# A four-layer graph network on one core: the attention of batch 13 is put behind the scores of batch 14

## The chip, the core and the metric

The kernel runs on one core of a Trainium2 chip. A core has a matrix engine (PE, with its weight loads PEld), a vector engine (DVE), an activation engine (ACT), a general engine (POOL) and a synchronizing engine (SP), which here only issues transfers. Each engine takes its instructions in the order in which the program lists them; between engines, semaphores say what has to wait for what. Transfers are issued from SP and from POOL and are run by 16 DMA engines. The metric is the device time in microseconds (us) of one execution; given is the median of several.

## The reference, cut to what matters

128 graphs of 128 nodes with 128 features pass through four graph layers, each `x = x + layer(relu(layernorm(x)), adj, ...)`. The change concerns the first layer only:

```python
D = jnp.abs(x[:, :, None, :] - x[:, None, :, :])
h = jnp.einsum('bijc,oc->bijo', D, W1) + b1
m = jnp.mean(h, axis=(0, 1, 2)); v = jnp.mean((h - m) ** 2, axis=(0, 1, 2))
h = _leaky((h - m) / jnp.sqrt(v + EPS) * g1 + be1)
s = jnp.einsum('bijo,uo->biju', h, W2)[..., 0] + b2[0]
A = jax.nn.softmax(jnp.where(A_init > 0, s, NEG), axis=-1)
y = jnp.einsum('bij,bjc->bic', A, x) @ Wg.T + bg
mg = jnp.mean(y, axis=(0, 1)); vg = jnp.mean((y - mg) ** 2, axis=(0, 1))
y = _leaky((y - mg) / jnp.sqrt(vg + EPS) * gg + beg)
out = jnp.concatenate([x, y], axis=2) @ Wt.T + bt
```

For every pair of nodes of a graph a hidden vector is computed and normalized over all pairs of all graphs; its score goes through a softmax over the neighbours. The result `y` is normalized over all nodes of all graphs. So there are two points at which everything before must be done: the statistics of `h`, and those of `y`. The three layers that follow are graph attention layers without such a point.

## The kernel before, in words

The two statistics cut the kernel into three stages.

**Stage one** computes, for each graph, the hidden values of all pairs (tile `v`, 128 x 4064) and their statistics, and stores `v` in DRAM; the last eight graphs' stay on the chip.

**Stage two**, where the change is, works in batches of eight graphs (`GS`): 16 batches, of which batch 15 comes first (its `v` are on the chip), and then 0 to 14. So batch 13 is the last but one, and batch 14 the last. A batch has these parts:

- `graph_scores`, for each graph: load `v` (L677, SP queue, 2 MB), affine and leaky on two halves of it (L657 on ACT, then L428 on DVE), a relu `r` of its last quarter (L664, ACT), and ten products on PE (L702) that add the graph's scores into the batch's PSUM tile `sc`. A graph's products come after those of the graph before; the last one's end is the event `("scores", k)`.
- `score_table`: it waits for that event. DVE copies `sc` to `us` (L721, two instructions), POOL issues four transfers of it to DRAM (`s<-us`, L731), and then one that reads it back in another layout (`u<-s`, L742), which waits for the four to land. Then two chains of `attention` are started, one for each four graphs (`GB`; called A and B here).
- `edges`, for each four graphs: load the adjacency (`adj`, L753, POOL queue) and the hidden features (`ht`, L761, SP queue), make the mask `negm` (L757, DVE), count edge types (L774, ACT), and `zg`, the features times Wg (`pz` on PE, L765, copied by ACT, L768).
- `attention`: one addition on POOL (L784); six products into `pl` (L791 to L794, PE; the last takes `negm`); maximum and difference (`mx`, `e`, L799 and L801, DVE); exp (L803, ACT); sum, reciprocal and scaling (`sm`, `ri`, `e`, L806 to L809, DVE); transposes `pt` (L813, PE), copied to `eT` (L816, ACT); products with `zg` into `py` (L820, PE); bias into `yt` (L823, ACT); a store of `yt` (L825, POOL queue); its statistics (L830 and L831, DVE).

When all batches' statistics are there, `y_norm` makes `y_sc` and `y_bi` (L382 to L420). `edge_types` puts the number of edge types seen into `types` (L849 to L857). After the stage every engine reads `types` and branches on it (L1349); SP can do so as soon as `types` is written, as it has nothing else to do, and then issues the first loads of the third stage (L1030).

**Stage three** computes the rest of layer one and layers two to four, four graphs at a time. Each group's first step applies `y_sc` and `y_bi` to the loaded `y` (`yl`, L1139).

**What sets the order.** Each part is a generator that yields its next step with the engine, an estimate of its duration, and the buffers that it takes and frees. `in_order` walks through all parts that are under way (up to ten in stage two) with a clock of its own: of all steps that could go next it takes the one that could begin first by its estimates, and of equals the part that was started first (once all parts have been started: the one started last). The order in which it takes them is the order of each engine's instructions, and stays fixed. A step can yield `"after"` with the name of an event: it is then not taken before this event is there, by the planner's clock. This is no wait on the chip by itself; it only moves the step in the lists. The transfers of SP and of POOL stand in the lists of these engines in the same way.

By this order, PE's list in the tail of stage two reads: scores of batch 14, graphs 0 to 4; `pl` of batch 13, A; graph 5; `pl` of batch 13, B; graph 6; a `pz`; graph 7; then the rest of batch 13's attention, and batch 14's.

Of the kernel before, what the change touches and what calls it, by code (L numbers as in the profile page):

```python
# [24 lines left out]
GS = 8  # L25
GB = 4
# [129 lines left out]
def bcast(ap, pos, n):  # L156

    dims = [list(d) for d in ap.ap]
    return bass.AP(tensor=ap.tensor, offset=ap.offset, ap=dims[:pos] + [[0, n]] + dims[pos:])
# [3 lines left out]
def kernel(ctx: ExitStack, tc: tile.TileContext, x, adj, w, out):  # L163
    nc = tc.nc
    NB = x.shape[0]
# [267 lines left out]
    with tc.tile_pool(name="h_pool", bufs=1) as h_pool, tc.tile_pool(name="pairs", bufs=B_V) as b_v:  # L433
# [193 lines left out]
        with tc.tile_pool(name="b2", bufs=2) as b2p, tc.tile_pool(name="b_s", bufs=2, space=PSUM) as b_s, tc.tile_pool(  # L627
            name="b_ps", bufs=6, space=PSUM
        ) as b_ps:
            scores, masks = {}, {}  # L630
# [80 lines left out]
            def score_table(k):  # L711

                yield "after", ("scores", k)
                yield DVE, 1.6, "us", "sc"
                sc = scores.pop(k)
                sd = scores_d[k % 2]
                us = b2p.tile([P, 512], F32, tag="us", name="us")
                for s in range(2):
                    n = 8 * width[2 * s]
                    half = slice(64 * s, 64 * s + 64)  # L720
                    nc.vector.tensor_scalar(  # L721
                        us[half, 0:n], sc[half, 0:n], b2_rows[half, :], None, ALU.add
                    )
                yield POOL, 2.6, "u u", ""
                u = b2p.tile([P, GS, W], F32, tag="u", name="u")
                for q in range(NQ):
                    skewed = bass.AP(
                        tensor=sd.tensor, offset=sd.offset + QR * q * ROW + 1,
                        ap=[[W + 1, QR], [4 * ROW, 8], [1, width[q]]],
                    )  # L730
                    nc.gpsimd.dma_start(  # L731
                        skewed,
                        us[QR * q : QR * q + QR, 0 : 8 * width[q]].rearrange(
                            "p (r j) -> p r j", r=8
                        ),
                    )
                yield "wait", 3.0
                yield POOL, 1.2, "", "us"
                by_row = bass.AP(
                    tensor=sd.tensor, offset=sd.offset, ap=[[ROW - 1, P], [W + 1, GS], [1, W]]  # L740
                )
                nc.gpsimd.dma_start(u, by_row)  # L742
                yield "wait", 8.0
                for g in range(GS // GB):
                    yield "fork", attention(k * GS // GB + g, u[:, g * GB : g * GB + GB, :])
                yield "join",

            def edges(g):
# [29 lines left out]
                if not to_see:  # L778
                    yield "done", "types"

            def attention(g, u):
                flat = "p g j -> p (g j)"
                yield POOL, 0.6, "", ""
                nc.gpsimd.tensor_tensor(  # L784
                    u[:, :, 0 : W - P], u[:, :, 0 : W - P], u[:, :, P:W], ALU.add
                )
                yield "after", ("edges", g)
                yield PE, 3.0, "pb", "u negm"
                negm, zg = masks.pop(g)
                pl = b_ps.tile([P, GB, P], F32, tag="pb", name="pl")  # L790
                nc.tensor.matmul(pl, ident, u[:, :, 0:P], start=True, stop=False)  # L791
                for i in range(GB):
                    nc.tensor.matmul(pl[:, i, :], u[:, i, 0:P], ident, start=False, stop=False)
                nc.tensor.matmul(  # L794
                    pl.rearrange(flat), ident, negm.rearrange(flat), start=False, stop=True
                )
                yield DVE, 1.4, "e", "pb"
                mx = b2p.tile([P, GB], F32, tag="mx", name="mx")
                nc.vector.tensor_reduce(mx, pl, AX.X, ALU.max)  # L799
                e = b2p.tile([P, GB, P], F32, tag="e", name="e")  # L800
                nc.vector.tensor_tensor(e, pl, bcast(mx, 2, P), ALU.subtract)  # L801
                yield ACT, 0.65, "", ""
                nc.scalar.activation(e, e, AF.Exp)  # L803
                yield DVE, 1.7, "", ""
                sm = b2p.tile([P, GB], F32, tag="sm", name="sm")
                nc.vector.tensor_reduce(sm, e, AX.X, ALU.add)  # L806
                ri = b2p.tile([P, GB], F32, tag="ri", name="ri")
                nc.vector.reciprocal(ri, sm)
                nc.vector.tensor_tensor(e, e, bcast(ri, 2, P), ALU.mult)  # L809
                yield PE, 0.7, "pb", "e"  # L810
                pt = b_ps.tile([P, GB, P], F32, tag="pb", name="pt")
                for i in range(GB):
                    nc.tensor.transpose(pt[:, i, :], e[:, i, :], ident)  # L813
                yield ACT, 0.65, "eT", "pb"
                eT = b2p.tile([P, GB, P], F32, tag="eT", name="eT")
                nc.scalar.copy(eT, pt)  # L816
                yield PE, 1.0, "pb", "eT zg"
                py = b_ps.tile([P, GB, P], F32, tag="pb", name="py")
                for i in range(GB):
                    nc.tensor.matmul(py[:, i, :], zg[:, i, :], eT[:, i, :], start=True, stop=True)  # L820
                yield ACT, 0.7, "yt", "pb"
                yt = b2p.tile([P, GB, P], F32, tag="yt", name="yt")
                nc.scalar.activation(yt, py, AF.Identity, bias=bg)  # L823
                yield POOL, 0.7, "", ""
                nc.gpsimd.dma_start(y_d[g], yt)  # L825
                yield "done", ("stored", g)
                yield DVE, 1.5, "", "yt"
                y6 = b2p.tile([P, GB, 6], F32, tag="y6", name="y6")
                for i in range(GB):
                    nc.vector.bn_stats(y6[:, i, :], yt[:, i, :])  # L830
                nc.vector.bn_aggr(y_mv[:, g, :], y6.rearrange("p a b -> p (a b)"))  # L831
                to_norm.remove(g)
                if not to_norm:
                    yield "done", "y"
# [37 lines left out]
            ]  # L872
            makers = []

            for k in [NB // GS - 1, *range(NB // GS - 1)]:
                of_edges = [partial(edges, k * GS // GB + g) for g in range(GS // GB)]
                order = sorted(range(GS * k, GS * k + GS), key=lambda b: b not in here)
                of_graphs = [partial(graph_scores, order, i) for i in range(GS)]

                n = 0 if makers else 2  # L880
                makers += of_graphs[:n] + of_edges + of_graphs[n:] + [partial(score_table, k)]
# [484 lines left out]
def program(arrays):  # L1366

    import concourse.bacc as bacc

    nc = bacc.Bacc("TRN2", target_bir_lowering=False, num_devices=1)  # L1370
    ins, aps = {}, {}
    for name in ["x", "adj"] + _WEIGHTS:
        a = arrays[name]
        ins[f"in_{name}"] = a
        aps[name] = nc.dram_tensor(
            f"in_{name}", a.shape, mybir.dt.from_np(a.dtype), kind="ExternalInput"
        ).ap()
    out = nc.dram_tensor("out_0", arrays["x"].shape, F32, kind="ExternalOutput").ap()
    with tile.TileContext(nc) as tc:
        kernel(tc, aps["x"], aps["adj"], aps, out)  # L1380
    return nc, ins
# [10 lines left out]
```

## Time and profile before

| | us |
|---|---|
| median of the runs | 3127.03 |
| lowest and highest of the three runs | 3125.08, 3133.86 |
| the profiled execution, its own time | 3131.72 |
| its span, first to last instruction | 3129.9 |
| stage two: first score product | 1257.8 |
| last score product of batch 14 ends | 2014.6 |
| `y_bi` done, stage three begins | 2052.0 |

The profile has start times from the start of the span. Each line of a timeline gives start, duration, engine, source line, operation, output and input, how many instructions are merged in the line, and in brackets how long the engine had been idle before it and what released it. Line numbers (L791) are those of the kernel before. The chain that ended last is followed back from the last instruction, at each step to what released it; in it, a name such as `DMA u<-s` stands for the time in which a transfer was waited for, and "issue" for time in which an engine waited for nothing that the profile shows. A clock of 1.00 is the full TensorE clock.

Busy over the span: PE 91%, DVE 85%, ACT 84%, POOL 48%. These shares are means over three stages with different limits, so they don't say what an edit at the end of the second is worth.

### The profile page before, as it was taken

The numbers are of one execution on the slowest core, as the hardware profiler recorded it, in microseconds if no ns is written. First come the engines' busy times: TensorE is split into PE (matmuls) and PEld (weight loads), VectorE is DVE, ScalarE is ACT, GpSimd is POOL, SyncE is SP. The second block draws the span as 40 slices with busy tenths as digits, with TensorE's granted clock in tenths as the row PEclk, the third lists the DMA queues.
The fourth block names the chain that finished last, engine by engine and source line by source line (L and its number), as shares of the span: only waits on it lengthen the run. The fifth ranks groups of instructions, "written<-read, shape, count | busy, mean of one in ns | idle before, by whom it ended". The sixth has DMA issues, their size and how long they took to land. (4 is left out here: it accounts for less than half of the span.)

```text
span 3129.9 us, 47376 instructions
## 1 busy us (share of the span) xinstructions
PE 2852.8 (91%) x17526; PEld 1588.3 (51%) x17577; DVE 2656.4 (85%) x4730; ACT 2626.3 (84%) x3050; POOL 1494.6 (48%) x953
## 2 busy tenths in 40 slices
PE   6999999999999999787988888879999999999997
PEld 2444434333443333233333333367877777787776
DVE  6999999999999999776877877667787787787886
ACT  4999999999999998887877878657777877787786
POOL 5999999999999997111111111121222222222202
PEclk8999999999999999898999999989999999999999
DMA  3555555555555651899999999620111111111000
GB/s 120 241 239 240 242 239 244 227 227 244 236 227 228 252 224 41 351 393 381 402 405 406 397 409 400 227 75 11 45 48 35 48 38 45 41 38 42 18 1 22
DMA packets 150722, 606.53 MB, mean 194 GB/s; under 512 B 15633, under 2 KB 99026, under 8 KB 119762
## 3 DMA queue, kind: packets, MB, share of 16 engines
q1 hardware_dynamic: 140242, 569.86, 46.0%
q0 software_dynamic: 10240, 33.53, 3.0%
q8 instruction: 143, 2.34, 0.3%
q14 instruction: 97, 0.79, 0.1%
HBM read 322.74 MB, written 280.61 MB: 193 GB/s over the span
## 5 line engine op out<-in xcount | busy, mean ns | idle before, releaser
L552 POOL TENSOR_TENSOR d<-he 128x2016 f32<-128x2016 f32 (+1 forms) x288 | 1021.6, 3573 | 68.1 <-PE ph L569 62.2
L569 PE MATMUL ph<-d,w1T 128*64 128x512 f32 (+1 forms) x4096 | 927.5, 595 | 36.5 <-DVE d L549 17.6
L555 ACT ACTIVATE d<-d 128x2016 f32<-128x2016 f32 (+1 forms) x352 | 675.0, 1921 | 13.1 <-POOL d L552 13.0
L584 DVE BATCH_NORM_STATS2 six<-v 128x6 f32<-128x512 f32 (+1 forms) x1024 | 624.6, 670 | 5.6 <-ACT v L579 5.4
L569 PEld LDWEIGHTS ph<-d,w1T 128*64 128x64 f32 x4096 | 308.0, 136 | 546.2 <-issue 397.3
L579 ACT COPY v<-ph 128x1008 f32<-128x1008 f32 (+1 forms) x512 | 509.6, 1028 | 30.7 <-PE ph L569 27.9
L549 DVE TENSOR_TENSOR d<-he,pt 128x2048 f32<-128x2048 f32 (+1 forms) x224 | 505.5, 2257 | 2.6 <-PE ph L569 2.3
L939 POOL TENSOR_TENSOR rs<-ve,nhalf 128x4 f32<-128x4 f32 x96 | 119.1, 1241 | 738.6 <-DVE ve L936 480.4
L428 DVE SCALAR_TENSOR_TENSOR v<-v 128x1528 f32<-128x1528 f32 x256 | 434.0, 1742 | 34.2 <-ACT v L657 33.5
L657 ACT ACTIVATE v<-v,h_bi,h_sc 128x1528 f32<-128x1528 f32 x256 | 413.2, 1664 | 6.7 <-DVE h_bi L420 6.7
L702 PE MATMUL sc<-v,w_slide 128*32 128x512 f32 (+1 forms) x1536 | 322.6, 601 | 17.2 <-DVE v L428 16.9
L1095 PE MATMUL pa<-vals,p 128*128 128x99 f32 (+2 forms) x2048 | 253.2, 279 | 11.3 <-DVE p L966 7.7
L1095 PEld LDWEIGHTS pa<-vals,p 128*128 128x128 f32 x2048 | 248.5, 197 | 29.1 <-DVE p L966 11.3
L702 PE MATMUL sc<-v,w_line 128*32 128x504 f32 x512 | 261.0, 592 | 0.0
L702 PE MATMUL sc<-r,w_relu 128*32 128x504 f32 x512 | 259.1, 588 | 0.0
L966 DVE SCALAR_TENSOR_TENSOR p<-p,q 128x1024 f32<-128x1024 f32 (+1 forms) x192 | 206.7, 1083 | 48.5 <-ACT q L1082 24.4
L569 PE MATMUL ph<-both,us 128*64 128x512 bf16 x1920 | 236.4, 379 | 0.0
L569 PEld LDWEIGHTS <-us 128*64 128x64 bf16 x1920 | 124.4, 110 | 147.5 <-issue 91.6
L1081 ACT ACTIVATE p<-z 128x1024 f32<-128x1024 f32 x128 | 133.2, 1041 | 35.2 <-PE z L962 34.8
L664 ACT ACTIVATE r<-v,h_bi,h_sc 128x1008 f32<-128x1008 f32 x128 | 157.6, 1231 | 0.0
L702 PEld LDWEIGHTS sc<-v,w_slide 128*32 128x32 f32 x1536 | 65.1, 109 | 160.1 <-DVE v L428 83.3
L803 ACT ACTIVATE e<-e 128x512 f32<-128x512 f32 x32 | 20.2, 631 | 141.0 <-DVE e L801 141.0
(255 smaller groups left out, 4505.4 us busy)
## 6 DMA issues: line engine op xcount, KB each, us to landing
v<-v SPq DMA_DIRECT2D x240, 2032.0 KB, 8.9
xg<-in_x SPq DMA_DIRECT2D x64, 256.0 KB, 3.0
ht<-h SPq DMA_DIRECT2D x64, 256.0 KB, 6.3
u<-s POOLq DMA_DIRECT2D x16, 768.0 KB, 11.7
h<-he SPq DMA_DIRECT2D x32, 256.0 KB, 2.6
adj<-in_adj SPq DMA_DIRECT2D x32, 256.0 KB, 2.9
adj<-in_adj POOLq DMA_DIRECT2D x32, 256.0 KB, 7.5
y<-yt POOLq DMA_DIRECT2D x32, 256.0 KB, 6.2
```

The lines of the kernel that those rows point to most:

```text
L428: engine.scalar_tensor_tensor(out, v, slope, v, ALU.mult, ALU.max)
L549: nc.vector.tensor_tensor(dv, later, own, ALU.max if larger else ALU.subtract)
L552: nc.gpsimd.tensor_tensor(dv, later, own, ALU.subtract)
L555: nc.scalar.activation(d[:, 0 : 4 * n], d[:, 0 : 4 * n], AF.Abs)
L569: nc.tensor.matmul(ph[64 * a : 64 * a + 64, t, 0:n], wt, x_, start=part == 0, stop=not larger or part == 3,)
L579: nc.scalar.copy(v.rearrange("p (t e) -> p t e", t=2), ph[:, :, 0:n])
L584: nc.vector.bn_stats(made["six"][:, 2 * q + t, :], v[:, t * n : t * n + n])
L657: nc.scalar.activation(part, part, AF.Identity, bias=h_bi, scale=h_sc)
L664: nc.scalar.activation(made["r"][:, 0:n], part, AF.Relu, bias=h_bi, scale=h_sc)
L702: nc.tensor.matmul(sc[rows, 0:n], wz[:, 31 - k : 63 - k], z, start=begins and q < NQ, stop=ends and q != NQ - 1, tile_position=(0, rows.st ...
L966: nc.vector.scalar_tensor_tensor(p, p, FLOOR, q, ALU.max, ALU.max)
L1095: nc.tensor.matmul(pa_all[:, h * (DH + 1) : h * (DH + 1) + n], p[:, h, :], vals_all[:, e : e + n], start=True, stop=True,)
```

## The change

`attention` now gets the number of its batch. For the last batch but one in the order of the list (`batches[-2:-1]`, batch 13) its first step yields `"after"` with the event `("scores", 14)`. The planner then takes no step of batch 13's two attention chains before it has taken the last score product of batch 14.

```diff
-                    yield "fork", attention(k * GS // GB + g, u[:, g * GB : g * GB + GB, :])
+                    yield "fork", attention(k, k * GS // GB + g, u[:, g * GB : g * GB + GB, :])
...
-            def attention(g, u):
+            def attention(k, g, u):
                 flat = "p g j -> p (g j)"
+                if k in batches[-2:-1]:
+
+                    yield "after", ("scores", batches[-1])
                 yield POOL, 0.6, "", ""
...
-            for k in [NB // GS - 1, *range(NB // GS - 1)]:
+            batches = [NB // GS - 1, *range(NB // GS - 1)]
+            for k in batches:
```

What this does to the engines' lists, all in the tail of stage two:

- PE: the score products of batch 14's graphs 5, 6 and 7 now come without a gap behind those of graph 4. Behind them come `pl` A, `pl` B, a `pz`, `pt` A, the small transpose of `edge_types`, the other `pz`, `py` A, `pt` B, `py` B, and then batch 14's `pl`, as before.
- DVE: the 14 `v` instructions of graphs 1 to 7 now come without a gap, then the two `us`, and only then `negm`, `mx`, `e` and the rest of batch 13's attention. `types` now comes behind `us` and behind `e` of B.
- ACT: one exchange: `eT` of A now stands ahead of `exp` of B.
- POOL: batch 14's `u<-s` now stands ahead of the store of batch 13's `yt` A, and batch 14's two additions ahead of the store of `yt` B.
- SP: the early load of `y` for stage three's first group and one load of `ht` change places.

The lists of stage one and of stage three are the same as before.

## The prediction

> **What bounds the kernel now.** I read first the busy times by stage (busy us and instruction counts of PE, PEld, DVE, ACT, POOL; then granted clock, DMA share, GB/s).
>
> ```profile
> 1257.80:2052.00 794.20, 664.00 (x3585) 271.87 (x3585) 590.80 (x654) 629.47 (x573) 117.76 (x175) 0.92 0.94 372
> 2052.00:3129.90 1077.90, 1004.64 (x7437) 823.39 (x7488) 851.30 (x2304) 830.21 (x1472) 238.98 (x320) 0.97 0.12 36
> ```
>
> Stage two is bound by its loads of v (DMA 0.94), but the last of them is issued at 1978, so its tail is not. I therefore went to the chain that ended last (start, us, what), around the end of stage two:
>
> ```profile
> 1997.32 1.05 PE pl L791 x2
> ...
> 2003.65 1.05 PE pl L791 x2
> ...
> 2009.97 1.09 PE pz L765 x8
> 2011.06 3.52 PE sc L702 x17
> ...
> 2020.85 0.43 issue
> 2021.28 8.63 DMA u<-s
> ...
> 2030.76 2.08 PE pl L791 x2
> ```
>
> Batch 13's `pl` and a `pz` stand between the last three graphs' `sc` products of batch 14. When those end (2014.58), batch 14's table still has to go to DRAM and back, and PE starts its attention only at 2030.76. Stage three waits for all of it: every `yl` needs `y_bi`, at 2051.99. The timelines of ACT, DVE and POOL say what else could hold the last products:
>
> ```profile
> 2001.16 3.23 ACT L657 ACTIVATE v<-v,h_bi,h_sc 128x1528 f32<-128x1528 f32 x2
> ...
> 1998.65 3.58 DVE L428 SCALAR_TENSOR_TENSOR v<-v 128x1528 f32<-128x1528 f32 x2 [0.28 <-ACT v L657]
> 2003.93 3.40 DVE L428 SCALAR_TENSOR_TENSOR v<-v 128x1528 f32<-128x1528 f32 x2
> 2014.62 1.53 DVE L721 TENSOR_SCALAR us<-sc,b_rows 64x512 f32<-64x512 f32 x2 [3.81 <-PE sc L702]
> 2016.49 0.14 DVE L857 CAST types<-odd 1x1 int32<-1x1 f32 x1
> ...
> 1989.62 0.89 POOL L742 DMA_DIRECT2D u<-s  x1 [7.68 <-DMA s<-us]
> 1995.08 3.88 POOL L784 TENSOR_TENSOR u<-u 128x256 f32<-128x256 f32 x2 [4.57 <-DMA u<-s]
> 2015.66 2.31 POOL L731 DMA_DIRECT2D s<-us  x4 [16.70 <-DVE us L721]
> 2021.28 0.90 POOL L742 DMA_DIRECT2D u<-s  x1 [1.24 <-PE py L820]
> 2029.98 1.40 POOL L784 TENSOR_TENSOR u<-u 128x256 f32<-128x256 f32 x2 [7.07 <-DMA u<-s]
> ```
>
> ACT runs without a gap to 2005.38, so it is the next limit on the scores. The read of u takes 5.46 us on idle DMA engines (1989.62 to 1995.08) and 8.7 us (2021.28 to 2029.98) beside stage three's first loads, which start at 2017.68, once `types` is written. Last the clock, in windows laid on its transitions:
>
> ```profile
> 2017.90:2021.33 3.43, 1.83 (x13) 1.39 (x12) 1.39 (x6) 2.10 (x4) 0.71 (x3) 1.00 0.69 144
> 2021.33:2024.74 3.41, 0.00 (x0) 0.00 (x0) 1.14 (x5) 0.72 (x2) 1.42 (x2) 1.00 0.91 282
> 2038.39:2041.80 3.41, 1.47 (x11) 1.26 (x12) 2.61 (x6) 1.13 (x2) 0.00 (x0) 1.00 0.00 0
> ```
>
> After the second and third of these the clock is at half; after the first it stays full. Between PE busy 1.47 and 1.83 of 3.41 us lies the point that decides.
>
> **What the Trainium skill says.** "TensorE: Matmul & The Clock Gate", Part 1: the PE clock halves after an idle window of about 3.4 us, and the window is free-running. The trace agrees: transitions at 1949.64, 1959.88, 2024.74, 2034.98 and 2041.80 are whole multiples of 3.41 us apart, and the four products of L791 to L794 took 4.95 us in the half-clock start at 2030.76, 2.87 us at 2003.58. The same page, Part 1, has ScalarE, VectorE and GpSimd as strict FIFO queues: the order written is the order run. "SBUF — State Buffer", SBUF: two separate sides: a VectorE operation with two SBUF inputs and a GpSimd operation that reads SBUF exclude each other. Here the two adds of L784 took 3.88 us under DVE work, 1.40 with DVE idle. "DMA: Bandwidth & Descriptors", Issuing engines are not separate DMA queues: all queues share 16 engines; the 5.46 against 8.7 us above fit.
>
> **The change, part by part.** No instruction is added or removed: each engine's list has the same members, and only the last 120 or so of stage two move. In stage three nothing moves.
>
> *PE.* Both `pl` groups (spacing 2.82 and 2.81 us) and one `pz` (1.09) go behind the last `sc`: 6.7 us less ahead of it. But DVE and ACT limit this. DVE loses `negm`, `mx`, `e` (1.78 us) ahead of the last pair of `v`. ACT's order there is unchanged, its last pair runs 2001.16 to 2004.39; so DVE's pair runs from 2002.87, for its 3.40, to 2006.27. From the second half of v to the next graph PE took 3.32 us where it stalled (1983.60 to 1986.92). 2006.31 + 3.32 = 2009.63, where 2014.51 was: **4.88 us earlier**. The graphs before stall for under 1 us each.
>
> *The round trip.* DVE's `us` now directly follows the last `v`, so it blocks `negm`, `mx`, `e` of batch 13 until 2011.29. As before, s is issued 1.04 us after `us` begins, and u 6.66 us after (2014.62 to 2021.28): 2009.74 + 6.66 = 2016.40. u now goes before the store of y26 on POOL. `types` is written behind batch 13's softmax start, at 2019.3 (below), so stage three's loads start at about 2020.4. The read of u then has the engines mostly alone: 5.5 us, 2021.9; with DVE busy the first add takes 0.7 to 1.9, so u is ready at 2022.6 to 2023.8. y26's store waits for `yt` at 2020.7 and so holds the add back only if `yt` is over 1 us late.
>
> *Attention of batch 13*, now whole behind the scores. `pl` A to 2012.50, `pl` B to 2015.32. The second `negm` reuses a buffer that `pl` B reads, and waits for it: 2015.37. `sm` of A 2015.70; from there as 2007.58 to 2010.81 before: `e` of B done at 2018.93. Then `types` 2019.2 to 2019.3, `exp` of B to 2019.60, `sm` of B 2019.65. `sm` to the end of `py` took 4.28 us (2016.56 to 2020.84), the next product can start about 0.15 before that end: **2023.8**. PE takes batch 14's `pl` in its order after this `py`. So PE starts it at 2023.8, 6.96 us earlier; u is ready by then, and this serial chain, not u, sets it.
>
> *From there to stage three.* PE now has gaps of 0.8 to 1.5 us, not 9.9. At full clock the first `pl` is released after 2.87 us, not 4.95: 2.08 more, `mx` at 2026.68 against 2035.72. Its way to `y_bi` is unchanged (16.27 us): 2042.95. **Gain 9.04 us.** Stage three's twelve loads are 2.7 us later against its start 9 us earlier; they were done 17.1 us after the first issue (2034.8), so by about 2037.5, 5 us ahead of need. That cover gone, each us of delay would cost one.
>
> *SP* swaps yt0 and one `ht` (0.37 and 0.43 us to issue, at 1978): nothing, since the `pz` that needs ht comes over 30 us later.
>
> Sum against the execution's own 3131.72: 3122.7. That execution is 4.7 over the median of the runs, so on the median: 3127.03 - 9.04 = 3118.0.
>
> What the trace of before doesn't show is the clock's phase. Boundaries fall anywhere; in a window ending between 2022.2 and 2023.7 PE is busy 1.17 of 3.41, under the point that decides, which is 1.5 of 3.41 phases. Then `pl` begins at half clock for 1.8 to 3.3 us and loses 0.9 to 1.7, with up to 0.6 more on `py`; a full loss gives back 2.08. On the other side, batch 14's second `pt` and `py` ran at half clock (1.11 and 2.08 us); at full (0.63 and 1.16) 1.4 us more is won. I take the middle: full at `pl`, half at the end; both ends stay for the range.
>
> **The rivals.**
> *Full clock to the end:* 9.04 + 1.4 = 10.4 us, 3116.6. For it: PE has no long gap any more; against it: the window of 1.47 after `pl` keeps its shape.
> *Half clock at pl again:* 7.0 us or somewhat less, 3120. For it: the 1.17 above.
> *u stays the wait:* if u takes 8.6 us although the loads start later, it lands at 2025.1, `pl` begins at 2025.9; with a cold clock the gain is 4.9, the scores' lead alone, 3122. Against it: `types` is behind u's issue by 2.9 us.
> *The order isn't felt:* if ACT or DVE already set the scores' end; against it PE is busy all 17.26 us from 1997.25.
> *Slower:* stage three runs its 1077.9 us at clock 0.97; that is (0.03 x 2 x 1077.9) / 3.41, about 19 half-clock windows, and a new start moves all windows against the work. Each more costs up to 1.7 us. From six more (10.2) it is slower than before; from eleven (18.7) by over 0.3%. Against it: the three runs, with phases of their own, differ by 8.8 us in all.
>
> **How the numbers follow.** Forecast (full at `pl`, half after; its own range 7.5 to 9.4 us) 0.45; full to the end 0.38; half at `pl` 0.07; u 0.04; not felt 0.02; slower 0.04. 0.3% is 9.4 us, about what a measurement of this kernel can tell from no change, and the forecast lies 0.4 us below it. So scatter of some 2 us moves 0.16 of the forecast's 0.45 over it and 0.09 of the faster case's 0.38 below: faster 0.45, within 0.51, slower 0.04. The range takes in u's case with 2 us of scatter (3124.5) and the full clock with 4.6 (3112).
>
> **What would show it.** Right: DVE's two `us` at about 2009.7, directly after the last `v` pair; u's issue at 2016.4 and its add at 2022; batch 14's `pl` at 2023.8, released by PE's own order and not by the add; `types` after `us`; `yl` at about 2043; stage three as long as before. Wrong: an add that ends after 2024, `pl` still at 4.95 us, or a stage three that differs from 1077.9 us by more than 3.

## The result and the profile after

| | before | after |
|---|---|---|
| median of 14 runs each, us | 3130.47 | 3121.31 |
| lowest and highest | 3122.76, 3136.57 | 3111.39, 3129.66 |
| the profiled execution: own time, span | 3131.72, 3129.9 | 3125.32, 3123.4 |

The ratio after to before is 0.9971, with a 95% interval from 0.9959 to 0.9983. On 3130.47 us that is 9.1 us less, from 5.3 to 12.8. The forecast of 9.04 us less lies in the middle of it; the forecast time, 3118.0, is 3.3 us under the median because the kernel before was itself 3.4 us slower in these runs (3130.47) than in the three runs shown first (3127.03).

First the busy times by stage of the kernel after, with the columns as for the kernel before (PE, PEld, DVE, ACT, POOL; granted clock, DMA share, GB/s):

```profile
1257.80:2045.60 787.80, 662.11 (x3585) 270.99 (x3585) 590.97 (x654) 629.81 (x573) 117.65 (x175) 0.92 0.95 375
2045.60:3123.40 1077.80, 1003.99 (x7437) 823.92 (x7488) 851.51 (x2304) 830.43 (x1472) 239.15 (x320) 0.98 0.12 36
```

Stage three is as long as before (1077.80 against 1077.90). All that changed is stage two: 6.4 us shorter between these two executions. The tail itself won more than that, and the profile shows why the difference is smaller. The timeline of ACT gives both ends of the tail:

```profile
2004.85 3.22 ACT L657 ACTIVATE v<-v,h_bi,h_sc 128x1528 f32<-128x1528 f32 x2
...
2045.61 2.93 ACT L1143 ACTIVATE yl<-yt,y_bi,y_sc 128x512 f32<-128x512 f32 x4 [4.19 <-DVE y_bi L420]
```

The last pair of `v` of batch 14 starts at 2004.85, where it was 2001.16. ACT's order ahead of it is the same in both kernels, and the pair starts anywhere from 1995.89 to 2007.11 in the four profiles of this study in which every list ahead of it is that of the kernel before (in the other eight, from 1999.05 to 2008.47). So these 3.69 us cannot be put down to the change: stage two ahead of its tail is bound by its loads, and its length varies by itself. I therefore measure every kernel below from this pair to the first `yl`, and call that **the tail**. Before it is 50.88 us (2001.16 to 2052.04), after 40.76: **10.12 us less**. The first `yl` of the kernel before:

```profile
2052.04 2.93 ACT L1139 ACTIVATE yl<-yt,y_bi,y_sc 128x512 f32<-128x512 f32 x4 [4.19 <-DVE y_bi L420]
```

What fills the tail now is seen in the chain that ended last (start, us, what):

```profile
2010.02 3.58 PE sc L702 x16
2013.60 1.05 PE pl L794 x2
...
2019.06 0.43 DVE negm L757
...
2022.66 0.64 ACT e L806
2023.32 0.70 DVE sm L809
...
2025.09 0.64 PE pt L816 x4
...
2026.39 1.16 PE py L823 x8
2027.55 0.86 PE pl L794 x2
...
2030.20 0.70 DVE mx L802
...
2045.61 0.82 ACT yl L1143
```

There is no `DMA u<-s` in it any more. From the last score products it goes through `pl`, the second `negm`, and batch 13's softmax of chain B to its `py` at 2026.39, and straight on to batch 14's `pl`. The timelines of DVE, POOL, SP and PE have the steps:

```profile
2013.64 1.52 DVE L721 TENSOR_SCALAR us<-sc,b_rows 64x512 f32<-64x512 f32 x2 [3.67 <-PE sc L702]
2022.85 0.14 DVE L860 CAST types<-odd 1x1 int32<-1x1 f32 x1
2020.17 0.91 POOL L742 DMA_DIRECT2D u<-s  x1 [3.15 <-DMA s<-us]
2025.20 0.58 POOL L828 DMA_DIRECT2D y<-yt  x1 [4.12 <-ACT yt L826]
2025.79 1.42 POOL L787 TENSOR_TENSOR u<-u 128x256 f32<-128x256 f32 x2
2023.91 0.39 SPq L1034 DMA_DIRECT2D xg<-in_x  x1
2026.39 1.16 PE L823 MATMUL py<-eT,zg 128*128 128x128 f32 x8 [0.67 <-ACT eT L819]
2027.39 1.02 PE L794 MATMUL pl<-u,ident 128*128 128x512 f32 x2
```

The `pl` at 2027.39 has no bracket: PE did not wait for u, it came to it in its own order. The first addition was held by the store of y26 (2025.20) and not by a transfer, as it too shows no wait for u, which had landed 5.3 us after its issue, at 2025.5. And the clock in windows laid on its transitions, to within 0.1 us (PE busy, clock, DMA share, GB/s):

```profile
2021.66:2025.07 3.41, 2.03 (x19) 1.00 0.78 235
2025.07:2028.48 3.41, 2.71 (x17) 1.00 0.86 244
2028.48:2031.89 3.41, 3.41 (x21) 1.00 1.07 357
2031.89:2035.30 3.41, 1.51 (x7) 1.00 1.09 363
2035.30:2038.71 3.41, 3.15 (x12) 0.51 0.33 114
```

PE has enough work up to `pl` for the clock to stay full. The window with 1.51 us of work is the one between `pl` and `pt`, and the next, with batch 14's first `py` (2.08 us), is at half.

### The profile page after: what moved, and what is told of

Same layout as the page of the kernel before. It is cut to its first block, busy times and chain, and to the rows that moved or that the text cites. A ratio compares the mean times of both kernels' runs of the same rounds, so it can differ in the third digit from the quotient of the medians.

```text
span 3123.4 us, 47377 instructions
## 1 busy us (share of the span) xinstructions
PE 2850.6 (91%) x17526; PEld 1587.6 (51%) x17577; DVE 2656.6 (85%) x4730; ACT 2626.8 (84%) x3050; POOL 1495.1 (48%) x953
## 4 chain that ended last, share of the span: by engine, by line
PE 27%; DVE 13%; issue 6%; ACT 5%; DMA 2%; POOL 1%; POOLq 0%; DVEq 0%; another core or an unknown queue 0%; ACTq 0%
PE pa L1099 6%; PE sc L702 4%; DMA s<-us 2%; PE po L1014 2%; DVE p L970 2%; PE ps L1118 1%; PE pp L1111 1%; PE pl L794 1%; PE z L966 1%; PE ph L1241 1%; PE pl L796 1%; DVE s L936 1%; DVE xh L1023 1%; PE pl L797 1%; DVE f1d L1202 1%
## 5 line engine op out<-in xcount | busy, mean ns | idle before, releaser
L1086 ACT ACTIVATE q<-z 128x1024 f32<-128x1024 f32 x128 | 133.6, 1044 | 0.0
```

## The experiments

The theory: `pl` of batch 14 waits for batch 13's serial chain, no longer for u; u is ready because the loads of stage three start behind its issue; and some 2 us of the gain are the clock. The rivals: the clock is most of it; or the late loads are most of it; or u still is the wait. All times in the table are from the last pair of `v`; "u read" is from the issue of u to the first addition that uses it, which may wait for other things too. Each tail is that of one execution.

| kernel | u issued | u read | batch 14's `pl` | `mx` | tail | ratio to before, 95% |
|---|---|---|---|---|---|---|
| before | 20.12 | 8.70 | 29.60 | 34.56 | 50.88 | |
| the change | 15.32 | 5.62 | 22.54 | 25.35 | 40.76 | 0.9971 (0.9959 to 0.9983) |
| change_again | 15.73 | 5.33 | 22.61 | 27.02 | 43.34 | 0.9964 (0.9949 to 0.9979) |
| change_once_more | 15.11 | 6.95 | 22.83 | 25.75 | 41.67 | 0.998 (0.997 to 0.999) |
| before_types_late | 19.68 | 5.90 | 26.35 | 30.69 | 47.00 | 0.999 (0.9977 to 1.0003) |
| before_pe_filled | 20.29 | 8.72 | 29.78 | 32.70 | 47.70 | 0.9986 (0.9972 to 1.0001) |
| before_both | 19.60 | 5.96 | 26.33 | 29.25 | 44.26 | 0.9979 (0.9967 to 0.999) |
| half_b_waits | 17.46 | 8.39 | 26.64 | 30.92 | 47.25 | 0.9988 (0.9977 to 0.9999) |
| change_loads_early | 15.77 | 10.08 | 26.63 | 32.15 | 47.10 | 0.9991 (0.9977 to 1.0006) |
| change_chain_longer | 14.95 | 5.98 | 26.67 | 30.67 | 46.08 | 0.9994 (0.9982 to 1.0005) |
| change_filled | 15.14 | 5.86 | 22.48 | 25.29 | 40.30 | 0.9953 (0.994 to 0.9967) |
| change_filled_longer | 15.23 | 5.70 | 22.47 | 25.28 | 40.30 | 0.997 (0.996 to 0.9979) |

The intervals of the whole times reach some 3 to 5 us to either side, as wide as most of the effects; what tells the kernels apart is the columns of the profile ahead of them. The tail moves with the phase of the clock: the change's own three executions lie between 40.76 and 43.34. The start of `pl` is steadier, 22.54 to 22.83 in the three.

### Stage three's loads alone: before_types_late

The kernel before, with the write of `types` put off until chain B of batch 13 is stored in the planner's order. SP's loads then start at 20.60 after the pair, where they started at 16.52; PE's order of scores and `pl` is that of before.

```diff
                 nc.tensor.transpose(pt, odd_p, ident)
+                yield "after", ("stored", 27)
                 yield DVE, 0.5, "", "pb"
```

> The kernel before, with nothing moved but the write of types, which now comes on DVE behind batch 13's last statistics (about 2023 us instead of 2016.6), so that stage three's loads start some 6 us later, after u's read has been issued. My theory: u's read meets the loads only with its tail and takes 5.5 to 6.5 us instead of 8.7, pl of batch 14 begins 2.2 to 3.2 us earlier, still at half clock: 47.7 to 48.7 us from the last pair of v to yl, and the time falls by 2 to 3 us. Rival (u's read is not slowed by the loads, only by its own small packets): 8.7 us as before, 50.9 us, no change; if the loads now arrive late for stage three, more.

From the timeline of POOL:

```profile
2026.79 0.90 POOL L742 DMA_DIRECT2D u<-s  x1 [0.80 <-PE py L820]
...
2032.69 1.40 POOL L784 TENSOR_TENSOR u<-u 128x256 f32<-128x256 f32 x2 [3.83 <-DMA u<-s]
```

The read takes 5.90 us in place of 8.70. That is 2.80 of the 3.25 us by which `pl` starts earlier; the rest is u's issue, which came 0.44 us earlier (19.68, not 20.12); the stores of `s` that it waits for landed after 2.8 us in the median, not 3.2. The tail is 3.88 shorter, a little more than expected: the half-clock start of `pl` was 0.62 shorter too (4.34 from `pl` to `mx`, 4.96 before). So loads that start ahead of the read of u cost it some 2.8 us in the kernel before, with no score moved.

### The clock alone: before_pe_filled, and both: before_both

The kernel before with products of the identity by itself, into a PSUM tile that nobody reads, behind batch 13's last `py`. They fill most of PE's gap of 9.9 us and add nothing to the result. (The profile shows each such product as two records, so 38 as x76.) Before_both has the two edits, with 24 products.

```diff
                     nc.tensor.matmul(py[:, i, :], zg[:, i, :], eT[:, i, :], start=True, stop=True)
+                if g in {27: 38}:
+                    fill({27: 38}[g])
...
+            def fill(n):
+                t = b_ps.tile([P, P], F32, tag="pb", name="fill")
+                for _ in range(n):
+                    nc.tensor.matmul(t, ident, ident, start=True, stop=True)
```

> The kernel before, with 38 products of the identity (8.4 us at full clock, result unused) on PE behind batch 13's last py, in the 9.9 us in which PE waits for u. Nothing else moves. My theory: the clock is at full when pl of batch 14 begins, the first pl is released after 2.9 us instead of 4.95, and mx comes 2.1 us earlier after the add: 48.8 us from the last pair of v to yl. Rival (pl is slow at its start for another reason, such as the weights or the wait itself): 4.95 us again, 50.9 us, or more by what the products delay pl.

> The kernel before, with both of these edits and 24 products instead of 38 (5.3 us): types late and PE filled, attention of batch 13 where it was. My theory: the two terms add, 5.3 us less: 45.5 us from the last pair of v to yl, and the time falls by about 5 us; what the changed kernel has beyond that (40.8) is the earlier scores less the serial chain. Rival (the whole gain of the changed kernel is the order on PE): no more than 1 us.

From the timeline of PE in before_pe_filled:

```profile
2023.47 8.65 PE L841 MATMUL fill<-ident 128*128 128x128 f32 x76
2033.74 1.13 PE L791 MATMUL pl<-u,ident 128*128 128x512 f32 x2 [1.62 <-POOL u L784]
```

`pl` waits for u as long as before (29.78 against 29.60), but its first pair takes 1.13 us where it took 2.08, and `mx` follows after 2.92 us in place of 4.96. The clock then also stays full for the `pt` and `py` after it: 15.00 from `mx` to `yl`, 16.32 before. In all 3.18 us, somewhat more than the 2.1 that the start of `pl` alone would give. The two edits together give 6.62; the sum of the two alone is 7.06, and 6.44 without the 0.62 of the shorter half-clock start, which it counts twice. They are two separate terms, and together the larger part of the 10.12 us. What neither gives is the rest: from before_both to change_filled (below), the change at full clock, the tail falls by another 3.96, of which 3.85 is `pl` starting earlier.

### Half of the wait: half_b_waits

Only chain B of batch 13 waits for the scores, chain A goes as before the change.

```diff
-                if k in batches[-2:-1]:
+                if k in batches[-2:-1] and g % 2:
```

> The changed kernel, with the wait only on the second of batch 13's two attention chains (B); A stays between graphs 4 and 5 as before. Measured from ACT's last pair of v in batch 14 to stage three's first yl: 50.9 us before, 40.8 after. My theory (four terms: earlier scores, a read of u that does not meet stage three's loads, less the serial chain, plus a full clock at pl): the scores' end is only about 2.8 us earlier, types is now written right after the table's two us, so stage three's loads start with u's read, which takes about 8.6 us again; PE then idles and pl begins at half clock, about 2.9 us earlier than before: 48 us. Rival (the loads do not matter to u, each us of earlier scores counts once or more): u lands after 5.5 us, pl 6 us earlier, 43 to 45 us. Time against before: theory 2 to 4 us less, rival 6 to 8 us less.

From the timelines of POOL and PE:

```profile
2018.47 0.90 POOL L742 DMA_DIRECT2D u<-s  x1
2026.27 0.57 POOL L828 DMA_DIRECT2D y<-yt  x1 [6.90 <-ACT yt L826]
2026.86 1.41 POOL L787 TENSOR_TENSOR u<-u 128x256 f32<-128x256 f32 x2
2027.65 2.08 PE L794 MATMUL pl<-u,ident 128*128 128x512 f32 x2 [2.88 <-POOL u L787]
```

The scores are done 1.7 us later than with the whole wait (`us` at 10.51, not 8.79), since `pl` of A is among them again. But that is the small part of the loss of 6.5 against the change's first profile. Batch 14's additions stand in POOL's list behind the store of chain B's `yt`, and this store is held to 2026.27. u itself is not what they wait for: it landed 5.9 us after its issue, at 2024.4. `pl`, released by the addition, then starts at half clock. So the tail came near the 48 us expected, but not for the reason expected: the read was to take 8.6 us again, and the loads, which start 0.7 us behind its issue, cost it little. With chain B alone held back, most of the gain is not had.

### Loads back to their early place: change_loads_early

The change, with `types` written right behind `us` again, by leaving edge types out of the count: the slice drops the last four groups, so those of batches 14 and 15.

```diff
-                yield "after", "types"
+                yield "after", ("scores", batches[-1])
...
-                nc.vector.tensor_reduce(odd_p, squares, AX.X, ALU.max)
+                nc.vector.tensor_reduce(odd_p, squares[:, 0 : n_parts - 4], AX.X, ALU.max)
```

> The changed kernel with types written right behind the two us, so that stage three's loads start about 7 us earlier (some 3 us ahead of u's read). The types of the last batch's two groups are left out of the count. My theory (u's read meets the loads as it did before the change): u takes about 8.5 us, pl of batch 14 begins 2 to 3 us later than in the changed kernel, released by the add and not by PE's own order, perhaps at half clock: 42.8 to 45 us from the last pair of v to yl, time 2 to 4 us more than the changed kernel's. Rival (the loads are done or make no difference): 40.8 us, no change.

From the timelines of SP, POOL and PE:

```profile
2015.72 0.39 SPq L1034 DMA_DIRECT2D xg<-in_x  x1
2019.65 0.91 POOL L742 DMA_DIRECT2D u<-s  x1 [3.61 <-DMA s<-us]
...
2029.73 1.40 POOL L787 TENSOR_TENSOR u<-u 128x256 f32<-128x256 f32 x2 [5.01 <-DMA u<-s]
2030.51 2.08 PE L794 MATMUL pl<-u,ident 128*128 128x512 f32 x2 [4.10 <-POOL u L787]
```

The loads now start 3.9 us ahead of u's issue. u is issued as early as in change_again (15.77), but takes 10.08 us instead of 5.33. So u is the wait again, and PE stands for 4.10 us. `pl` starts 3.8 to 4.1 us later than in the change's three executions, and at half clock, and the tail is 47.10, more than expected. Against the three (40.76, 41.67, 43.34) that is 3.8 to 6.3 us longer, and the clock's phase is in this difference; the delay of `pl` is what the loads account for. So the place of one write of four bytes in DVE's list, which starts SP's loads, decides over some 4 us of the gain, more where the clock falls badly.

### The chain made longer: change_chain_longer

The change, with the sum of chain B (`sm`) taken three times on DVE.

```diff
-                nc.vector.tensor_reduce(sm, e, AX.X, ALU.add)
+                for _ in range(3 if g == 27 else 1):
+                    nc.vector.tensor_reduce(sm, e, AX.X, ALU.add)
```

> The changed kernel with the sum of batch 13's chain B taken three times instead of once on DVE, 1.4 us more in the chain that runs from the scores' end to the last py of batch 13; u is not touched. My theory (this chain, in PE's order ahead of batch 14's pl, sets pl): pl 1.4 us later, 42.2 us from the last pair of v to yl. Rival (u's read or POOL's add sets pl): no change, 40.8 us.

From the timelines of DVE, POOL and PE:

```profile
2026.93 2.13 DVE L810 TENSOR_REDUCE sm<-e 128x4 f32<-128x512 f32 x3 [0.34 <-ACT e L806]
2029.31 2.06 DVE L813 TENSOR_TENSOR e<-e,ri 128x512 f32<-128x512 f32 x1
2029.40 1.41 POOL L787 TENSOR_TENSOR u<-u 128x256 f32<-128x256 f32 x2
2035.14 1.91 PE L794 MATMUL pl<-u,ident 128*128 128x512 f32 x2
```

u is ready as early as in the change (the additions at 20.93), and still `pl` starts 4.13 us later. So the chain sets it, and 1.4 us on the chain is not hidden. Of the 4.13, 1.44 are the two added sums. The next step, `e` times `ri`, took 2.06 us instead of 0.69, as it fell together with POOL's additions: 1.37 more. The remaining 1.3 lie on `pt` and `py`, which ran at half clock here, so the tail is 46.08 and not the 42.2 expected. The edit was meant to add one delay and added three, so it shows which way the wait goes, not its exact slope.

### The change twice more: change_again, change_once_more

> The changed kernel once more, beside the three that follow. My theory: 40 to 41.5 us from ACT's last pair of v to the first yl, whatever the phase of the clock, 8 to 10 us less time than before. Rival (the 9 us of the first comparison were partly the draw of stage two's loads): a difference under 6 us.

> The change a third time. Its tail, from the last leaky pair of batch 14 to the first yl, was 40.76 us in one execution and 43.34 in another, by where the clock's windows fell. If that is the phase alone: batch 14's pl starts 22.5 to 22.7 us after the pair again, and the tail is between 40.3 (full clock everywhere) and 43.5. If PE's start of pl differs by over 0.3 us, something besides the clock varies. Ratio to the kernel before 0.9955 to 0.998.

PE starts batch 14's `pl` at 22.54, 22.61 and 22.83 after the pair in the three executions. The last is 0.13 outside what was expected: there the read of u took until 22.06, and its addition, with 1.15 us of waiting for the transfer, became the later of the two by a little. The tails differ by 2.6 us, nearly all of it clock. The 43.34 of change_again misses what was expected for it, 40 to 41.5 us whatever the phase: the phase does matter. From change_again, the timeline of PE, and two windows around the start of `pl` (PE busy, clock, DMA share, GB/s):

```profile
2027.17 1.92 PE L794 MATMUL pl<-u,ident 128*128 128x512 f32 x2
2028.88 1.80 PE L796 MATMUL pl<-ident,u 128*128 128x128 f32 x8
```

```profile
2023.59:2027.00 3.41, 1.52 (x12) 1.00 0.92 267
2027.00:2030.41 3.41, 3.41 (x13) 0.50 0.98 323
```

The window that ends at 2027.00, 22.4 us after the pair, holds 1.52 us of PE work, and the clock is at half for the next one, just where `pl` starts. In the change's first profile the boundary lay at 20.2 (2025.07), and the window ahead of it held 2.03.

### PE filled in the change: change_filled, change_filled_longer

The change with 2 to 4 identity products in each gap of PE in the tail, and 20 (change_filled) or 31 (change_filled_longer) behind the last `py`.

```diff
+                fill({27: 4, 29: 4}.get(g, 0))
...
+                fill({27: 2, 28: 2, 29: 2}.get(g, 0))
...
+                fill({26: 4, 28: 2, 29: 20}.get(g, 0))
```

> The changed kernel with products of the identity on PE (results unused) in the gaps of the tail: 2 to 4 in each gap between the attention products of batches 13 and 14, 20 (4.4 us) behind the last py. No other instruction moves. My theory (the clock's windows are what makes the last pt, py and stage three's first products slow): pt and py at 0.63 and 1.16 us throughout, 0.5 to 1.4 us less to yl (39.4 to 40.3), and stage three's first po products 0.22 us apart instead of 0.43, up to 2 us more at stage three's start: 1 to 3 us less time than the changed kernel. Rival (stage three's start is set by DVE and by loads, and a product that is in the way costs as much as it brings): no difference or slower by up to 1 us.

> As change_filled, but 31 identity products instead of 20 behind the last py, so that PE has work until about 2.2 us after the first yl starts. If the near-empty window there was what put stage three's first po at half clock, the first po pairs are now 0.22 us apart, not 0.43 or 0.64, for about 1.5 us less; the tail stays at 40.2 to 40.5. If the filling delays stage three's first products, the first po comes later than 2.6 us after the first yl starts. Ratio 0.995 (0.9935 to 0.9965), at best 3 us ahead of the change itself.

All `pl`, `pt` and `py` now run at full clock, and the tail is 40.30 in both. In change_filled the first `po` of stage three still came 0.43 us apart. The windows of PE show why (PE busy, clock, DMA share, GB/s):

```profile
2034.90:2038.31 3.41, 3.41 (x33) 1.00 0.19 77
2038.31:2041.72 3.41, 1.20 (x11) 1.00 0.00 0
...
2041.90:2042.00 0.10, 0.07 (x1) 0.50 0.00 0
```

The 20 products ended too early. With 31, as expected, the `po` pairs are 0.22 to 0.32 us apart from the first at 2044.57 on, 2.30 after the first `yl`. In whole times that is not seen, and the ratio misses the 0.995 expected: run on one chip in the same rounds, change_filled_longer has 0.997 and the change 0.998, with intervals that overlap. The filled kernels beat the kernel before, and the shortest median of all is that of change_filled (3120.11 against 3125.84 for the change beside it, 0.9953 and 0.9964), but that either beats the change itself is not shown.

## Why the prediction was right

**The scores' end, 4.88 us earlier: right.** `us` starts 8.79 us after the last pair, where it was 13.46: 4.67. It is 8.77 to 8.79 in every execution in which both chains wait.

**u's issue, 6.66 us after the scores: right.** Predicted at 15.24 after the pair (2016.40 less 2001.16), measured 15.32. Two small misses offset each other here, 0.21 late at the scores and 6.53 in place of 6.66 from there, and in the other executions in which both chains wait the issue comes anywhere from 14.95 to 15.77. The read then took 5.3 us to land, with 5.5 forecast, and batch 14's additions were held by about 0.3 for the store of y26. The prediction had this store hold them only if `yt` came over 1 us late; it came 0.5 late (20.04 after the pair, not 19.54) and held them already, at no cost, since `pl` was not waiting.

**Batch 13's chain sets pl: right, to 0.1 us at each step.** From the pair, predicted and measured: second `negm` 14.21 and 14.21; end of `types` 18.1 and 18.14; SP's first load 19.2 and 19.06; `sm` of B 18.49 and 18.47; `pl` of batch 14 at 22.64 and 22.54. That it is the chain and not u is shown by change_chain_longer, where u was as early and `pl` late. But the margin is thin: in change_once_more u was the later one, by 0.2 to 0.3 us.

**The late loads as the condition: right, and more of the gain than the text made of it.** They stood in the working as a step that makes u ready in time. Change_loads_early shows that without them `pl` starts some 4 us later and the tail is 47.10, not 40.76 to 43.34, and before_types_late that they alone give 3.88, 0.62 of it clock. The rival "u stays the wait" was put at 4.9 us, with a read of 8.6. With the loads ahead of u the read takes 10.08, and 3.8 us of the gain are left. It was put aside for the right reason: `types` behind u's issue.

**The clock: the mechanism was right, the choice between its cases was luck.** The prediction took full clock at `pl` and half at the end, 9.04 us. The profiled execution had full clock at `pl`, half for batch 14's first `py` and second `pt` (2.08 and 1.11), and full for the last `py` (1.16), which had been at half: 0.92 of the 1.4 us that the "full to the end" rival had added. The other 0.17 came between the pair and `mx` (9.21 against 9.04). So 10.12 lies between the forecast and this rival. The other two executions gave 9.21, the forecast, and 7.54, the rival "half clock at pl again" (7.0 or somewhat less). That rival had been given 0.07, although the text itself had found that 1.5 of 3.41 phases lead to it. By that share it should have had some 0.4, or less for the part of `pl` that it touches; one execution of three is too few to say which.

The share itself rests on the reading that a window with less than 1.47 to 1.83 us of work halves the clock; that held for the windows of this tail, but it is no fixed point (see the last section). The kernel before was profiled once, so how its own tail moves with the phase isn't known.

Change_filled against before_pe_filled takes the clock out of the comparison: both ran at full clock, and the tail falls from 47.70 to 40.30. So 7.40 us belong to the order and the loads, with the clock full in both: 3.44 of them to the late loads (47.70 to 44.26, before_both) and 3.96 to the order (44.26 to 40.30). Up to 3.18 belong to the clock, which the kernel before loses on its gap of 9.9 us; the change gave back 0.46 of that in its first profile, and at most 1.37 and 3.04 in the other two. What the prediction calls the four products of L791 to L794 are six, as the list of the kernel's parts has them; the two durations that it reads there are right.

**Stage three: right.** 1077.80 us against 1077.90, and its first twelve loads were done well ahead of the first `yl` at 2045.61: the last was issued at 2032.4, and none took over 7.8 us to land. That `yl` waits for `y_bi` (4.19 us of idle time, ended by it). "Slower", by more half-clock windows, did not come.

**The whole time.** 3130.47 less 9.04 is 3121.43, and 3121.31 was measured. That is closer than the working deserves: the three measurements of the change give ratios from 0.9964 to 0.998, 11 to 6 us, and the clock's phase alone moves the tail by 2.6.

## What to carry to other kernels

At the end of a stage, look for work of an earlier batch that the order of the list alone puts in front of the last data: moved behind it, it fills the gap that a round trip through DRAM leaves. Then ask which transfers a moved instruction lets go, for here one small write on DVE opened SP's queue, and with these loads ahead of a read on the critical path some 4 us of the gain are lost. Where PE stands idle for some microseconds ahead of critical products, give both phases of the clock's windows their chance, and compare profiles from a common point inside the stage.

## What the runs showed of the hardware

**A window with some work also halves the clock.** The Trainium skill ("TensorE: Matmul & The Clock Gate", Part 1) speaks of an idle window. Here windows of 3.41 us in the tail that held 1.20, 1.36, 1.51, 1.52 and 1.64 us of modelled PE work at full clock were followed by half clock, and those with 1.83 and 2.03 were not. The 1.64 is from change_once_more, the window ahead of its half-clock `py` (PE busy, clock, DMA share, GB/s):

```profile
2033.21:2036.62 3.41, 1.64 (x12) 1.00 0.58 207
2036.62:2040.03 3.41, 2.52 (x12) 0.53 0.19 77
```

This is no fixed point, though, as the prediction takes it to be. In stage three of the kernel before, the window from 2977.06 to 2980.47 held 2.32 us by the same count and was followed by half clock, and the one from 3086.29 to 3089.70 held 1.55 and was not. What the clock goes by, if not the modelled busy time, stays open.

**Either of two engines can be the one that waits.** In the kernel before, DVE's work stretched POOL's pair of additions from 1.40 to 3.88 us; in change_chain_longer POOL kept its 1.41 and DVE's product went from 0.69 to 2.06. "SBUF — State Buffer", SBUF: two separate sides, has such a pair exclude each other, with the first to start going first. The run agrees on the first point and shows the DVE side of it. It does not show the second: in the profile DVE's product starts at 2029.31 and POOL's additions at 2029.40, and it was DVE that took longer.

**The read of u suffers from loads that start ahead of it, far more than from those that start behind it.** The same 768 KB took 8.6 us from issue to landing with the loads 3.6 us ahead of it (before) and 10.0 with them 3.9 us ahead (change_loads_early). With the loads 0.7 to 0.9 us behind its issue it took 5.8 to 5.9 (half_b_waits, before_types_late, before_both), and with them 3.3 to 4.1 us behind 5.2 to 5.3, in five executions of six. In the sixth, change_once_more, it took 6.9 with the loads 3.9 us behind, and why is not known; nor was it tried why the first two differ by 1.4 us at nearly the same lead. Work on DVE is not what slows it: DVE was busy for 1.14 of the 8.70 us of the kernel before, and for 4.77 of the 5.31 of change_again. "DMA: Bandwidth & Descriptors", Issuing engines are not separate DMA queues, says that all queues share the 16 engines; by how much a read suffers is what these runs add.
